# Two-layer attention kernel: sums of the last two blocks shared with VectorE, first two blocks without transferred taps, new order places

## The chip, the cores and the metric

The kernel runs on one core of one Trainium2 chip. The metric is device time in microseconds, as the median of several executions. The names used are those of the profile: PE is TensorE (PEld its weight loads), DVE is VectorE, ACT is ScalarE, POOL is GpSimd, and SP is the engine whose queue issues most of the DMAs.

## The reference, cut to what matters

The input x is a batch of 4 images of 192 channels and 128 x 128 pixels, in float32. Two layers follow each other.

The first layer makes four groups of 192 channels with a 1x1 convolution and a depthwise 3x3 convolution. It forms attention between channels (8 heads of 24 channels, sums over all pixels), applies it to the values, adds x and a gate that comes from the pooled fourth group, and projects with a 1x1 convolution.

The second layer is the one that the change touches:

```
x = x + depthwise3x3(x) + bias
q, k, v = 1x1 convolution of x          (3 dilations: 1, 2, 3; 2 heads of 32 channels each)
scores  = q . k at the 3x3 neighbours   (reflected at the edges, dilated)
weights = softmax over the 9 neighbours
out     = sum over the 9 neighbours of weight * v
out     = 1x1 projection of the three dilations together
```

## The kernel before, in words

The program has two passes. The first one projects x and stores q, k and v of the first layer, then computes the channel attention head by head on PE. The end of that part is the matrix `mix1`, `mix2` (attention and projection multiplied together). It ends in the profile at about 1638 us. The change leaves all of this as it is.

The second pass (`second_pass`) does the rest. Its work is cut into 64 blocks: a block n is 4 rows of 128 pixels of two images, which lie side by side in the 128 partitions where the channels need it. There are 32 blocks for each pair of images. For each block:

- `loads`: SP loads x and v of the first layer (buffers `xv`). `h_product` multiplies them on PE, `h_evict` moves the result from PSUM into ring buffers of 12 rows (`hboth`, `hring2`) on ACT.
- `plan_conv`: the depthwise 3x3 convolution. Channels 0 to 127 of both images lie in `hboth`. `centre` (ACT) makes the middle tap into a PSUM tile `pa`; six taps (`SUMMED` = 0, 1, 2, 6, 7, 5) are added one after the other on DVE (`tap`, line 924), and the last of them writes the tile `y`. The other two taps (`MOVED` = 3, 8) are made by ACT (`moved`, line 937) and added by two accumulating DMAs that POOL issues (`moved_sum`, line 949): the first adds one tap onto the other, the second adds both onto `y`. The remaining 64 channels of both images (`side`) are made by ACT as nine tiles, summed by two accumulating DMAs (`side_rows`, line 968) and two adds on POOL (`side_sum`, lines 976 and 979) into `y2`.
- `plan_kv` and `plan_scores`: k, v and q on PE. Every one of these takes a product with `y` first and then one with `y2`. ACT evicts k and v into rings (`kring`, `vring`). `prod` (line 1094) multiplies q and k on DVE, `pick_sums` (line 1105) sums over channels on PE.
- `plan_softmax`: a chain through ACT, PE, DVE and POOL that ends in a transposing DMA (`weights`, on SP) into `e_sb`.
- `plan_mixed`: for each of three dilations g and nine neighbours t, PE spreads the weights over the channels (`expand`, line 1227, into two PSUM buffers `ex`), DVE multiplies by v (`term`, line 1233: the first one of a group writes `acc`, the others one of four `term` buffers), and POOL adds the eight terms onto `acc` (`term_sum`, line 1236). Then PE projects (`out_product`, lines 1245 and 1249), ACT evicts and SP stores.

The order of all of this is planned before it is issued. Each step is handed to a `Schedule` with an engine, a rank, an estimated cost, and the steps that it must follow. `order()` plays the work through in time: whenever an engine is free, it takes the step of lowest rank among those that are ready, and the order in which steps are taken is the order in which instructions go into the queues. A rank is the block's number plus a place from the table `PLACES` (a first value, and a step for repeated operations), in blocks. A change of PE's tile shape costs 0.12 us in this plan, and such a step's rank is raised by a penalty (1.6704 blocks), so that equal shapes are taken together. The engines then run their queues in order, and every dependence is a semaphore wait.

Buffers limit how far a step can run ahead: `hold` makes the first use of a buffer wait for the last use of its earlier holder. In this pass there are four `term`, four `acc`, two `ex`, two `pc` (PSUM, used for h, k and v, and the output), and one `moved` and one `side` buffer.

Of the kernel before, what the change touches and what calls it, by code (L numbers as in the profile page):

```python
# [36 lines left out]
class Schedule:  # L37
# [16 lines left out]
    def hold(self, pool, bufs, first, last):  # L54

        self.pools.setdefault((pool, bufs), []).append((first, last))
# [130 lines left out]
def rows3(t):  # L187
# [13 lines left out]

PLACES = {
    "loads": (0.5697, 0),
    "h_product0": (-0.8250, 0),
    "h_evict0": (0.7179, 0),
    "h_product1": (-0.2901, 0),
    "h_evict1": (4.5043, 0),
    "h_product2": (-0.7755, 0),  # L210
    "h_evict2": (-0.2139, 0),
    "centre": (5.7183, 0),
    "tap": (2.8884, 0.19030),
    "moved": (-0.0827, 0),
    "moved_sum0": (3.1492, 0),
    "moved_sum1": (4.7398, 0),
    "side1": (1.2593, 0.00003),
    "side0": (0.7171, 0.00011),
    "side_rows0": (2.1868, 0),
    "side2": (1.6271, 0.00019),  # L220
    "side_rows2": (1.4785, 0),
    "side_sum1": (10.8296, 0),
    "side_sum2": (5.4172, 0),
    "kv0": (1.7866, 0.00185),
    "kvev0": (-0.0330, 0.01478),
    "kv1": (3.2540, 0.00019),
    "kvev1": (-2.0029, 0),
    "kv2": (2.4499, 0),
    "kvev2": (1.1258, 0),
    "query0": (2.8659, 0),  # L230
    "prod0": (2.9696, 0),
    "query1": (3.3887, 0),
    "prod1": (3.0988, 0),
    "query2": (3.4244, 0),
    "prod2": (3.5942, 0),
    "pick0": (3.5728, 0.17857),
    "pick1": (3.9636, 0),
    "evicted_scores": (1.8388, 0),
    "by_pixel": (3.8163, 0),
    "top": (6.6680, 0),  # L240
    "below": (5.0643, 0),
    "exponential": (10.6231, 0),
    "total": (-2.1855, 0),
    "divide": (3.8560, 0),
    "part0": (-5.1709, 0),
    "rest": (-2.3314, 0),
    "part1": (-0.0711, 0),
    "part2": (1.6351, 0),
    "weights": (12.2563, 0),
    "expand": (4.2596, 0),  # L250
    "term": (4.7246, 0),
    "term_sum": (8.9696, 0),
    "out0": (6.1072, 0.00004),
    "outev0": (6.1953, 0),
    "store0": (18.8924, 0),
    "out1": (6.1208, 0),
    "outev1": (7.1247, 0),
    "store1": (9.7231, 0),
}

@with_exitstack
# [549 lines left out]
def second_pass(tc, x, w2, xv_p, mix1, mix2, biases, v_dram, v2_dram, out):  # L811
# [4 lines left out]
    with ExitStack() as ctx:  # L816
# [7 lines left out]
            ),  # L824
            dict(pc=2, ex=2, q=1, pa=1, sc=1),
            dict(xv=xv_p),
            (0.12, 1.6704),
        )
        add, hold, tile_of, tiles = stage.schedule.add, stage.hold, stage.tile, stage.tiles
        fill, read, repeat, written = stage.fill, stage.read, stage.repeat, stage.written  # L830
# [12 lines left out]
            nc.gpsimd.memset(r[:, :, 0 : W + 2 : W + 1], 0.0)  # L843

        def at(name, n, k=0):
            first, step = PLACES[name]
            return n + first + step * k

        mm = nc.tensor.matmul

# [135 lines left out]
        def plan_conv(n):  # L986
            prev = first = add("ACT", at("centre", n), 1.25, (centre, n), latency=0.3)
            for m in range(2):
                read("h", m, n, 0, first)
            for j, t in enumerate(SUMMED):  # L990
                prev = add("DVE", at("tap", n, j), 1.19, (tap, n, t, j == 5), [prev])
                for m in range(2):
                    read("h", m, n, t // 3 - 1, prev)
            hold("pa", first, prev)
            two, mvs = prev, []
            for k, t in enumerate(MOVED):
                mvs.append(add("ACT", at("moved", n, k), 1.15, (moved, n, k, t), mvs[-1:]))
                for m in range(2):
                    read("h", m, n, t // 3 - 1, mvs[k])
            both = summed_by_transfer(at("moved_sum0", n), 4.0, (moved_sum, n, 0), mvs)  # L1000
            both = summed_by_transfer(at("moved_sum1", n), 4.0, (moved_sum, n, 1), [both, two])
            hold("moved", mvs[0], both)
            firsts, sums = {}, []
            for j, ty in enumerate((1, 0, 2)):
                for tx in range(3):
                    sd = add("ACT", at(f"side{ty}", n, tx), 0.72, (side, n, ty, tx), firsts.get(ty, [])[-1:])
                    read("h", 2, n, ty - 1, sd)
                    firsts.setdefault(ty, []).append(sd)
                if j:
                    after = [firsts[1][-1], firsts[ty][-1], *sums[-1:]]  # L1010
                    sums.append(summed_by_transfer(at(f"side_rows{ty}", n), 5.8, (side_rows, n, ty), after))
                    hold("side", firsts[ty][0], sums[-1])
            for tx in (1, 2):
                sums.append(add("POOL", at(f"side_sum{tx}", n), 1.26, (side_sum, n, tx), sums[-1:]))
            hold("middle", firsts[1][0], sums[-1])
            return [sums[-2], two, both, [both, sums[-1]]]
# [212 lines left out]
        def term(n, g, t):  # L1229
            ex = tiles.pop(("ex", n, g, t))  # L1230
            to = tile_of("term", ("term", n, g, t)) if t else tile_of("acc", ("acc", n, g))
            for win, px in windows(vring, RING_V, n, g, t):
                nc.vector.tensor_mul(rows3(to[:, px]), rows3(ex[:, px]), win)  # L1233

        def term_sum(n, g, t):
            nc.gpsimd.tensor_add(tiles["acc", n, g], tiles["acc", n, g], tiles.pop(("term", n, g, t)))  # L1236

        def out_product(n, m, g):

# [24 lines left out]
        def plan_mixed(n, w):  # L1264
            sums, spreads = [], []
            for g in range(NG):
                exs, prev = [], None
                for t in range(NT):
# [5 lines left out]
                    if t == 0:  # L1274
                        first = prev = tm
                        continue
                    prev = add("POOL", at("term_sum", n, k), 1.277, (term_sum, n, g, t), [tm, prev])
                    hold("term", tm, prev)
                spreads += exs
                sums.append((first, prev))  # L1280
# [167 lines left out]
```

## Time and profile before

| what | us |
|---|---|
| median of 3 runs | 4407.45 (4406.96 to 4409.0) |
| the profiled execution | 4406.01 |
| its span, first to last instruction | 4404.2 |
| PE busy in the span | 4289.9 (97%) |
| DVE busy | 3806.3 (86%) |
| POOL busy | 3319.0 (75%) |
| ACT busy | 2593.1 (59%) |

The busy time of an engine is the time in which it ran some instruction; issuing DMAs and waiting do not count. A wait in the profile is put down to what released it last. The chain of work that ended last follows the program back from its last instruction, at each step to what released it. In lists by time, a bracket at the end of a line tells how long the engine was idle before it, and what ended that.

### The profile page before, as it was taken

To read this page: it belongs to the slowest core of one execution; us is meant where nothing else is said; L and a number is where in the kernel's file an instruction comes from. 1 tells how busy PE (TensorE), PEld (TensorE's weight loads), DVE (VectorE), ACT (ScalarE), POOL (GpSimd) and SP (SyncE) were. 2 spreads that over 40 slices of the span, in tenths; PEclk is the share of its full clock that TensorE was granted. 3 is DMA by queue.
4 is the path that set the end of the run, shared out by engine and by line. 5 is a ranking of instruction groups with operands and counts; after the bars stand their busy time and mean duration, and the time that the engine had idled before them with its cause. 6 is when DMAs were issued, how large, how long until landed. Compare 5 with 4: busy or idle time off the path is not lost.

```text
span 4404.2 us, 64532 instructions
## 1 busy us (share of the span) xinstructions
PE 4289.9 (97%) x20608; PEld 1649.0 (37%) x20608; DVE 3806.3 (86%) x5492; ACT 2593.1 (59%) x4858; POOL 3319.0 (75%) x3407
## 2 busy tenths in 40 slices
PE   9999999899999998999999999999999999999996
PEld 3333333354445642333333333333333333333321
DVE  7998889855555546999999999999999999999996
ACT  7888888833333337656656556556566566566531
POOL 6777778811111112999999999999999999999998
PEclk9999999999999999999999999999999999999997
DMA  8777787668887648666566666656565665665521
GB/s 268 245 243 237 230 258 251 198 154 175 178 174 172 143 109 177 131 133 135 126 130 132 126 130 129 136 123 128 127 136 124 131 134 125 133 131 125 116 53 32
DMA packets 502386, 675.81 MB, mean 153 GB/s; under 512 B 138576, under 2 KB 320412, under 8 KB 502048
## 3 DMA queue, kind: packets, MB, share of 16 engines
q1 hardware_dynamic: 464160, 504.94, 43.2%
q0 software_dynamic: 37888, 166.74, 20.9%
q8 instruction: 166, 2.72, 0.3%
q14 instruction: 172, 1.41, 0.1%
HBM read 277.72 MB, written 201.33 MB: 109 GB/s over the span
## 4 chain that ended last, share of the span: by engine, by line
PE 80%; DVE 13%; issue 3%; POOL 2%; DMA 1%; ACT 1%; SPq 0%; DVEq 0%; POOLq 0%; ACTq 0%
PE pc L640 12%; PE sc L1105 9%; PE ex L1227 8%; PE pu L357 8%; PE ph L872 7%; PE pkv L1026 5%; DVE term L1233 4%; PE pu L362 4%; PE gram L712 4%; PE pkv L1029 4%; PE q L1086 4%; PE q L1083 4%; DVE prod L1094 3%; PE pu L490 2%; PE po L1249 2%
## 5 line engine op out<-in xcount | busy, mean ns | idle before, releaser
L1236 POOL TENSOR_TENSOR acc<-acc,term 128x512 f32<-128x512 f32 x1536 | 2034.6, 1330 | 133.0 <-DVE term L1233 45.5
L1233 DVE TENSOR_TENSOR term<-ex,vring 128x512 f32<-128x512 f32 (+2 forms) x1596 | 1000.1, 663 | 55.3 <-PE ex L1227 43.1
L1094 DVE TENSOR_TENSOR prod<-q,kring 128x1536 f32<-128x1536 f32 (+1 forms) x600 | 1007.3, 1688 | 16.8 <-PE q L1083 7.3
L427 POOL TENSOR_TENSOR v_True<-v_True,side 128x512 f32<-128x512 f32 (+1 forms) x512 | 647.9, 1267 | 169.7 <-ACT side L416 141.9
L404 DVE SCALAR_TENSOR_TENSOR pa<-vboth,dwv,pa 128x1024 f32<-128x1024 f32 (+1 forms) x448 | 574.3, 1282 | 76.9 <-ACT pa L397 54.4
L1227 PE MATMUL ex<-e_sb,spread 108*128 108x512 bf16 x1728 | 567.2, 387 | 37.5 <-DVE term L1233 31.2
L627 POOL COPY band<-band 64x384 f32<-64x384 f32 x192 | 95.8, 499 | 563.9 <-DMA band<-in_bands 506.5
L640 PE MATMUL pc<-u,band 64*64 64x508 f32 (+1 forms) x4608 | 518.3, 593 | 1.4 <-ACT ring L386 1.4
L1039 ACT COPY kring<-pkv 64x512 f32<-64x512 f32 x384 | 223.3, 581 | 419.5 <-PE pkv L1029 413.9
L924 DVE SCALAR_TENSOR_TENSOR pa<-hboth,posw,pa 128x1024 f32<-128x1024 f32 (+1 forms) x320 | 408.3, 1276 | 38.8 <-ACT pa L912 19.7
L1105 PE MATMUL sc<-prod,pick 128*32 128x512 f32 x3456 | 428.9, 598 | 1.8 <-DVE prod L1094 1.8
L653 DVE BATCH_NORM_STATS2 stats<-pc 128x6 f32<-128x128 f32 x1440 | 303.0, 283 | 141.1 <-ACT conv L649 141.0
L649 ACT COPY conv<-pc 128x512 f32<-128x512 f32 x384 | 210.6, 587 | 296.9 <-PE pc L640 288.7
L1026 PE MATMUL pkv<-y,wkv 128*128 128x512 f32 x768 | 365.5, 598 | 11.8 <-DMA y<-moved 8.7
L1227 PEld LDWEIGHTS <-spread 108*128 108x128 bf16 x1728 | 133.4, 98 | 647.0 <-issue 626.7
L872 PE MATMUL ph<-xv,mix 128*64 128x512 f32 (+1 forms) x1024 | 374.3, 596 | 0.5 <-DMA mix<-mixed 0.5
L357 PE MATMUL pu<-xt,wx 128*128 128x512 f32 x768 | 366.0, 613 | 8.3 <-DMA xt<-in_x 8.3
L1252 ACT COPY o<-po 128x512 f32<-128x512 f32 x192 | 106.2, 588 | 433.5 <-PE po L1249 227.9
L416 ACT ACTIVATE side<-ring,dwv 128x512 f32<-128x512 f32 (+1 forms) x512 | 350.8, 736 | 13.9 <-POOL v_True L427 13.1
L956 ACT ACTIVATE side<-hring,posw 128x512 f32<-128x512 f32 (+1 forms) x512 | 340.9, 710 | 9.6 <-DMA side<-side 7.7
L640 PEld LDWEIGHTS pc<-u,band 64*64 64x64 f32 x4608 | 189.5, 134 | 301.2 <-issue 284.7
L1039 ACT COPY vring<-pkv 64x512 f32<-64x512 f32 x384 | 223.9, 583 | 45.9 <-PE pkv L1029 32.6
(165 smaller groups left out, 6073.8 us busy)
## 6 DMA issues: line engine op xcount, KB each, us to landing
qk_dram<-us SPq DMA_DIRECT2D x192, 512.0 KB
u<-qk_dram SPq DMA_DIRECT2D x384, 256.0 KB
side<-side POOLq DMA_DIRECT2D x124, 768.0 KB, 7.1
xt<-in_x SPq DMA_DIRECT2D x64, 512.0 KB
v_dram<-v_False SPq DMA_DIRECT2D x64, 512.0 KB
xv<-in_x SPq DMA_DIRECT2D x128, 256.0 KB
xv<-v_dram SPq DMA_DIRECT2D x128, 256.0 KB
y<-moved POOLq DMA_DIRECT2D x64, 512.0 KB, 5.2
```

Source lines behind the costliest of these rows:

```text
L357: mm(pu, wx[:, mt * 128 : (mt + 1) * 128], tiles["xt", n][:, im, :], start=True, stop=False)
L404: nc.vector.scalar_tensor_tensor(by_row(to[:, o : o + length]), by_row(vboth[:, at : at + length, :, t % 3 : t % 3 + W]), dwv[:, 0, t : t ...
L427: nc.gpsimd.tensor_add(v[:, rows, :], v[:, rows, :], z[:, rows, :])
L640: nc.tensor.matmul(pcs[e][r * G : (r + 1) * G, :, to], band[at, e, c, dx, :], u[at, e, c, :].rearrange("p (b w) -> p b w", w=W)[:, :, of], ...
L872: mm(to, w[:, cols], tiles["xv", n, j, im], start=j == 0, stop=j == 2)
L1026: mm(rows3(tile_of("pc", key)), w, tiles["y", n, im], start=True, stop=False)
L1039: nc.scalar.copy(rows[HALVES[im], :, pad : pad + W], rows3(tiles["pkv", n, pair, im])[HALVES[e]])
L1094: nc.vector.tensor_mul(to[:, :, px].rearrange("p t (r w) -> p t r w", w=W), q.unsqueeze(1).to_broadcast([128, 3, *q.shape[1:]]), three,)
L1105: mm(sc[quad * 32 : (quad + 1) * 32, :], pick[:, QR - 4 * row : QR - 4 * row + 32], tiles["prod", n, k // NT, k % NT // 3][:, k % 3, :], s ...
L1227: mm(rows3(tile_of("ex", ("ex", n, g, t))), spread[:, t, :], e_sb, start=True, stop=True)
L1233: nc.vector.tensor_mul(rows3(to[:, px]), rows3(ex[:, px]), win)
L1236: nc.gpsimd.tensor_add(tiles["acc", n, g], tiles["acc", n, g], tiles.pop(("term", n, g, t)))
```

## The change

There are three parts, all in the second pass.

1. In blocks 0 and 1, the taps 3 and 8 are no longer made on ACT and added by transfers. DVE adds them between its fifth and its last tap, so it does eight taps there instead of six.
2. In blocks 62 and 63, the sums of the neighbours t = 6, 7 and 8 of each dilation are made on DVE instead of POOL (`helped`): 3 x 3 x 2 = 18 sums. The plan prices one at 0.60 us instead of 1.277.
3. All places in the table are replaced. Each gets two more values: for blocks 0 to 3 the first is added (4 - n) times, and for blocks 60 to 63 the second is added (n - 59) times. The penalty for a change of shape becomes 2.2447.

```diff
-    "loads": (0.5697, 0),
-    "h_product0": (-0.8250, 0),
-    "h_evict0": (0.7179, 0),
-    "h_product1": (-0.2901, 0),
-    "h_evict1": (4.5043, 0),
...
-    "tap": (2.8884, 0.19030),
-    "moved": (-0.0827, 0),
...
-    "side_sum1": (10.8296, 0),
-    "kv0": (1.7866, 0.00185),
-    "prod0": (2.9696, 0),
-    "evicted_scores": (1.8388, 0),
-    "below": (5.0643, 0),
-    "part0": (-5.1709, 0),
-    "rest": (-2.3314, 0),
-    "term": (4.7246, 0),
-    "term_sum": (8.9696, 0),
-    "store0": (18.8924, 0),
...
+    "loads": (3.2117, 0, -0.1081, -0.1768),
+    "h_product0": (-1.0791, 0, -0.2172, 0.0738),
+    "h_evict0": (-1.5681, 0, 0.4291, 0.7768),
+    "h_product1": (-0.4538, 0, -0.1272, -0.2531),
+    "h_evict1": (2.9139, 0, -1.1902, 0.4891),
...
+    "tap": (3.0287, 0.15354, -0.1279, -0.1148),
+    "side_sum1": (12.5101, 0, 0.4347, 0.0454),
+    "kv0": (1.6801, 0, 0.0023, -0.1926),
+    "prod0": (3.1190, 0, -0.0092, -0.0614),
+    "evicted_scores": (3.4729, 0, 0.2114, -0.4090),
+    "below": (3.6315, 0, 0.3421, -0.3529),
+    "part0": (-7.1206, 0, 0.7557, 0.1340),
+    "rest": (-4.3348, 0, -0.2530, -0.1376),
+    "term": (3.3951, 0, 0.2670, -0.1634),
+    "term_sum": (13.4212, 0, -0.3796, -0.0967),
+    "store0": (15.2417, 0, -0.7670, 0.0550),
+    "moved": (-0.1229, 0, 0.8936, -0.5433),
...
-            (0.12, 1.6704),
+            (0.12, 2.2447),
...
         def at(name, n, k=0):
-            first, step = PLACES[name]
-            return n + first + step * k
+            first, step, early, late = PLACES[name]
+            u = n + first + step * k
+            if n < 4:
+                u += early * (4 - n)
+            if 2 * NB - 1 - n < 4:
+                u += late * (4 - (2 * NB - 1 - n))
+            return u
...
-            for j, t in enumerate(SUMMED):
-                prev = add("DVE", at("tap", n, j), 1.19, (tap, n, t, j == 5), [prev])
+            early = n < 2
+            on_vector = SUMMED[:5] + MOVED + SUMMED[5:] if early else SUMMED
+            for j, t in enumerate(on_vector):
+                prev = add("DVE", at("tap", n, j), 1.19, (tap, n, t, t == SUMMED[5]), [prev])
...
-            two, mvs = prev, []
-            for k, t in enumerate(MOVED):
-                mvs.append(add("ACT", at("moved", n, k), 1.15, (moved, n, k, t), mvs[-1:]))
...
+            two, both, mvs = prev, prev, []
+            if not early:
+                for k, t in enumerate(MOVED):
+                    mvs.append(add("ACT", at("moved", n, k), 1.15, (moved, n, k, t), mvs[-1:]))
...
+        def helped(n, g, t):
+
+            return n >= 2 * NB - 2 and t >= 6
+
         def term_sum(n, g, t):
-            nc.gpsimd.tensor_add(tiles["acc", n, g], tiles["acc", n, g], tiles.pop(("term", n, g, t)))
+            engine = nc.vector if helped(n, g, t) else nc.gpsimd
+            engine.tensor_add(tiles["acc", n, g], tiles["acc", n, g], tiles.pop(("term", n, g, t)))
...
-                    prev = add("POOL", at("term_sum", n, k), 1.277, (term_sum, n, g, t), [tm, prev])
+                    engine, us = ("DVE", 0.60) if helped(n, g, t) else ("POOL", 1.277)
+                    prev = add(engine, at("term_sum", n, k), us, (term_sum, n, g, t), [tm, prev])
```

## The prediction

> **What bounds the kernel now.** I read the busy times by stretch first, then the chain that ended last, then both ends in order of time, then groups and waits. The stretches of the second pass (columns: length, then busy us and instructions of PE, PEld, DVE, ACT, POOL, then the granted PE clock, DMA share, GB/s):
>
> ```profile
> 1626.00:1800.00 174.00, 151.46 (x558) 50.44 (x558) 114.08 (x141) 120.59 (x225) 69.10 (x68) 0.94 0.71 155
> 1800.00:4200.00 2400.00, 2378.62 (x9970) 846.45 (x9968) 2361.97 (x2704) 1436.45 (x2806) 2260.06 (x1905) 1.00 0.61 129
> 4200.00:4280.00 80.00, 74.05 (x307) 23.65 (x309) 75.88 (x91) 27.90 (x67) 73.76 (x62) 0.96 0.21 46
> 4280.00:4391.00 111.00, 80.92 (x273) 22.78 (x265) 81.03 (x129) 12.32 (x27) 105.31 (x85) 0.79 0.11 29
> ```
>
> From 1800 to 4200 PE is busy 99.1% and DVE 98.4%. A block takes about 41.65 us there (three blocks lie between the ph products at 2063.88 and 2188.81 in the chain), so 2,400 us are 57.6 blocks with 0.37 us of PE idle each. The change takes no PE work away. All that a new order can win in the middle is 21.4 us, in practice much less, but it can lose any amount. At the ends PE idles 22.5 us in the first stretch, and the last two stretches hold 36 us. There the two structural edits act.
>
> The start, from the chain and from POOL's own list:
>
> ```profile
> 1660.29 1.29 DVE y L924
> 1661.60 1.22 ACT pa L912
> ...
> 1665.72 9.14 DMA y<-moved
> 1675.00 3.63 PE pkv L1026 x4
> 1678.63 1.06 PE pkv L1029 x4
> ```
>
> ```profile
> 1659.09 0.89 POOL L949 DMA_DIRECT2D moved<-moved  x1 [7.56 <-ACT moved L937]
> 1660.91 0.85 POOL L968 DMA_DIRECT2D side<-side  x1 [0.93 <-ACT side L956]
> 1665.72 0.85 POOL L949 DMA_DIRECT2D y<-moved  x1 [3.96 <-DVE pa L924]
> 1671.34 1.26 POOL L976 TENSOR_TENSOR y<-side 128x512 f32<-128x512 f32 x1 [4.76 <-DMA side<-side]
> 1672.68 1.26 POOL L979 TENSOR_TENSOR y<-y,side 128x512 f32<-128x512 f32 x1
> ```
>
> Block 0's y leaves DVE at 1661.6 but is complete only when the transfer lands at 1674.9; PE stands 8.68 us. Right behind it is a second path: the side channels (y2), summed by two transfers and two POOL adds, end at 1673.94.
>
> The tail, from POOL's list and the waits after 4280 (total us, times, longest):
>
> ```profile
> 4280.00 20.08 POOL L1236 TENSOR_TENSOR acc<-acc,term 128x512 f32<-128x512 f32 x15
> ...
> 4308.67 22.64 POOL L1236 TENSOR_TENSOR acc<-acc,term 128x512 f32<-128x512 f32 x17
> ...
> 4336.55 54.40 POOL L1236 TENSOR_TENSOR acc<-acc,term 128x512 f32<-128x512 f32 x41
> ```
>
> ```profile
> DVE term L1233 <- POOL acc L1236: 11.1, 18, 1.5
> ```
>
> POOL runs 79 sums and six softmax steps almost without a gap until 4390.95. DVE has slack (81.0 us busy) and waits for POOL to free term buffers. PE's last out products follow at 4391.0, and the rest to 4404.2 is a fixed 13 us.
>
> **What the Trainium skill says.** "SBUF — State Buffer", section "Who interferes with whom": a VectorE instruction with two SBUF inputs contends with a GpSimd instruction that reads SBUF, and the later one is held until the other ends. The second pass of the kernel before has no row where this meets: term and prod read one operand from PSUM (ex, q), tap reads pa there. So no run here shows it yet, and I bound it below. "GPSIMD Engine Reference", section "3. Performance versus the Vector engine", gives a two-input add as 1.96 times slower on GpSimd; here it is 1267 ns on POOL against 722 ns for the nearest VectorE row with SBUF operands, 1.75 times:
>
> ```profile
> L701 DVE TENSOR_TENSOR square<-cutT 128x512 f32<-128x512 f32 x8 | 5.8, 722 | 16.5 <-ACT cutT L699 16.5
> ```
>
> "TensorE: Matmul & The Clock Gate", section "What's actually happening": PE falls to half clock after an idle window. The trace agrees: after the 8.68 us wait four pkv matmuls take 3.63 us, in the middle 1.72.
>
> **The change, part by part.** The sum is made against the profiled execution, 4406.01 us (span 4404.2 and 1.8 around it); the median of the three runs is 1.44 above it.
>
> *First two blocks without transferred taps.* Removed: 4 ACT taps of 1.14 us (4.6), 4 accumulating transfers of 512 KB, 4 issues of about 0.87 us on POOL's queue (3.5). Added: 4 DVE taps of 1.28 us (5.1), bare DVE time in a stretch where DVE idles 60 us; without that cover they cost 5.1. y of block 0 is then ready near 1661.6 + 2 x 1.3 = 1664.2 instead of 1674.9, 10.7 earlier. That is not the gain, for y2 is late next: the second product of each pair (L1029) needs it, and behind that instruction PE's queue holds the other pairs and the queries. y2 is ready at 1673.94; the first ACT tap in front of the sides is gone (1.15), POOL's issue in front of side_rows is gone, and two transfers fewer share the DMA engines, which are over-full (share 1.07 from 1665 to 1675). I bound y2 between 1673.9 and 1669. The first pair's L1029 starts at 1678.56 before, so block 0 gains 4.6 to 9.5. Block 1 has its y<-moved issue at 1687.16 behind side_rows, and PE then waits 2.97 us at 1698.10 and runs slow again (3.00 instead of 1.72): up to 4 us more, at the least nothing. After that the ramp is paced by PE itself and by the first e_sb transpose at 1744.91, so a part is lost again. Bounds 3 and 13; I take **-7**.
>
> *Last two blocks' sums.* t = 6, 7, 8 of three groups and two blocks are 18 sums. POOL loses 18 x 1.34 (its pitch, 54.40/41 = 1.33, and the step) = 24.1 us. DVE gains 18 x 0.72 = 13.0. Upper end: without contention DVE holds 81.0 + 13.0 = 94.0 us from 4280, POOL 111.0 - 24.1 = 86.9, so DVE becomes the bound, the last sum ends no earlier than 4374, and 17 us are won at most. Lower end: with contention each DVE sum first lets POOL's running sum end (half of 1.27, 0.63), so DVE holds 81.0 + 18 x 1.35 = 105.3 and wins 5.7; POOL is held 13.0 and ends 11 earlier. Queued behind a waiting DVE sum are terms, which PE's expands (two ex buffers) wait for. The sums' place is 13.4 blocks behind their own, later than all other DVE work, so in the plan they fill DVE's holes and do not push terms. I take **-10**. If DVE had no holes, the 13.0 would stand on its path in full.
>
> *Order anew.* All places move and two get terms for four blocks at either end; the penalty for a change of PE's tile shape goes from 1.6704 to 2.2447. No instruction is added. In the middle most places stay near the old (kv, query, prod within 0.4 block), while h_evict1, below, evicted_scores, part0, rest, side_sum and term_sum move by 1 to 4.5. These are small ACT, POOL and DVE steps; on SP only loads and stores move (loads 2.6 blocks later, store0 3.7 earlier), and SP's queue is far from full. The trace cannot say what order comes out, so the bounds are -8 (PE's idle falls by a third) and +26 (0.45 us a block, worked out below). I take **0**.
>
> Sum: 4406.0 - 7 - 10 = 4389.0, as a median **4390.4, so 4390 us**.
>
> **The rivals.**
>
> *The middle loses its cover (slower).* PE's idle is 0.37 us a block because expand and term hand two ex buffers back and forth with hardly a stall: from 1800 to 4200 terms wait 29.0 us for expands and expands 13.5 for terms. If the new places put one more prod (1.66 us) ahead of a due term, the next expand and what stands behind it on PE wait. At 17/57.6 = 0.30 us a block the gain of both ends is gone; at 0.45 the time is 4406 - 17 + 26 = 4415, a median of 4416. For it: three engines over 94% busy. Against it: the heavy places hardly moved.
>
> *Moved sums give nothing.* DVE sums stand for POOL and POOL for them, terms come late, and the tail's gain is 0 to 4. Then only the start is left: 4406 - 7 - 2, a median of 4398. For it: both operands lie in SBUF. Against it: DVE waits for POOL there anyway, so some of its standing is free.
>
> *Both ends at their full worth.* -12 at the start, -17 at the tail, -6 in the middle: 4371, a median of 4372. For it: separate end places. Against it: DVE would need to be full from 4280 on.
>
> *The ends' edits do not act.* Were y not on PE's path, the start would give nothing, but the chain shows the transfer there; this is within the cases above.
>
> **How the numbers follow.** Forecast 0.54 (own range 4380 to 4398), moved sums worthless 0.18, full worth 0.11, middle slower 0.17. Within 0.2% is 8.8 us, 4398.6 to 4416.3: what a measurement of this kernel can hardly tell from none. The forecast gives 0.49 faster and 0.05 same; worthless sums 0.09 and 0.08 and 0.01 slower; full worth 0.11 faster; the slow middle 0.02 same and 0.15 slower. Together 0.69, 0.15, 0.16. The range 4368 to 4413 takes in the full worth and most of the small losses.
>
> **What would show it.** Start: no y<-moved before block 2, PE's wait before the first pkv under 3 us or moved to L1029, first expand near 1747 instead of 1753.7. Tail: 18 POOL sums fewer and 18 acc<-acc,term rows on DVE; their mean tells the contention (0.72 is none, 1.35 the lower end); last sum 6 to 17 us nearer to the steady stretch's end. Middle: PE idle of 0.9% as before. The prediction is wrong if PE's idle in the middle passes 1.6% (0.30 us a block more), or if DVE sums last over 2 us.

## The result, and the profile after

The changed kernel takes 4411.48 us (median of 13 runs, 4408.91 to 4415.85) against 4407.45 us for the kernel before on the same chip (13 runs): a ratio of 1.001, with a 95% interval of 1.0001 to 1.0019. By the bound of 0.2% that is no change; the interval lies above 1, so what difference there is, about 4 us, is a loss. The forecast was 4390, with a range up to 4413. The expected gain of 17 us did not arrive.

The profiled execution of the changed kernel took 4415.85 us (span 4414.1), 9.9 more in span than before. Of these, 3.3 lie in the first pass, which the change leaves alone: the last row of the channel attention's sums over pixels (`gram`) starts at 1609.09 instead of 1605.82. Over all profiled executions of this study this start spreads by 5.3 us, though no kernel changes anything before it. So below all starts are "net", that is, less the difference to the kernel before.

The busy times by stretch of the changed kernel (columns as in the prediction: length, then busy us and instructions of PE, PEld, DVE, ACT, POOL, then clock, DMA share, GB/s):

```profile
1626.00:1800.00 174.00, 157.32 (x590) 53.42 (x589) 121.30 (x146) 114.05 (x214) 63.82 (x62) 0.94 0.63 141
1800.00:4200.00 2400.00, 2378.16 (x9919) 842.32 (x9917) 2347.14 (x2689) 1419.45 (x2791) 2248.86 (x1895) 1.00 0.60 128
4200.00:4280.00 80.00, 75.34 (x314) 25.05 (x313) 77.32 (x92) 33.67 (x82) 76.84 (x64) 1.00 0.30 62
4280.00:4401.00 121.00, 90.68 (x320) 25.20 (x320) 104.04 (x160) 16.54 (x36) 98.43 (x77) 0.81 0.12 30
```

The first row shows the gain at the start: PE is busy 157.3 instead of 151.5 us. The last one, which like the one before it ends with the last sum, shows the tail's edit: DVE works 104.0 instead of 81.0 us, POOL 98.4 instead of 105.3 (some of it work that was done before 4280 in the kernel before). In the second row PE's share is the same 99.1% as before, but fewer PE and DVE instructions fit into the same 2400 us (9919 and 2689, instead of 9970 and 2704). So the middle is slower, and PE's idle time doesn't show it.

To see it, one must hold the work constant, not the time. A good mark is DVE's first softmax step of a block (`mx<-st`). Between those of blocks 11 and 54 lie 43 blocks, in the kernel before and in the one after:

```profile
2186.58:3977.79 1791.21, 1774.28 (x7440) 632.11 (x7439) 1761.05 (x2028) 1072.09 (x2094) 1685.63 (x1420) 1.00 0.62 130
```

```profile
2187.27:3986.67 1799.40, 1783.72 (x7441) 632.23 (x7441) 1759.61 (x2028) 1064.46 (x2094) 1685.20 (x1420) 1.00 0.60 129
```

The same number of instructions of DVE, ACT and POOL takes 8.2 us longer, 0.19 a block in the mean. DVE and POOL work no longer on them, but PE is "busy" 9.4 us longer with the same number of matmuls (one record in 7440 apart).

From mark to mark the profiled execution of after stands to before like this (us):

| stretch | before | after | difference |
|---|---|---|---|
| last `gram` row to block 9 | 497.03 | 494.48 | -2.55 |
| block 9 to block 57 | 1999.25 | 2009.23 | +9.98 |
| block 57 to block 63 | 223.55 | 226.80 | +3.25 |
| block 63 to the end of the span | 78.55 | 74.50 | -4.05 |

Both ends gain, though less than half of what was forecast, and the stretch between takes all of it back.

At the start, PE's own list for the changed kernel (the lines left out don't wait):

```profile
1667.28 1.08 PE L1095 MATMUL q<-y,wq 128*64 128x512 f32 x4 [1.02 <-DVE y L930]
...
1673.29 1.12 PE L1092 MATMUL q<-y,wq 128*128 128x512 f32 x2 [0.26 <-POOL y L985]
1674.35 1.13 PE L1038 MATMUL pkv<-y,wkv 64*128 64x512 f32 x4
1677.92 1.17 PE L878 MATMUL ph<-xv,wp 128*128 128x512 f32 x2 [2.44 <-ACT kring L1048]
```

The wait of 8.68 us for the transfer onto `y` is gone. What is left are 1.02 us for DVE's `y`, 0.26 for POOL's `y2`, and 2.44 for ACT, which evicts k and v. The first pair's second product (now L1038) starts at 1674.35, net 1671.1, instead of 1678.56: 7.5 us earlier.

In the tail, POOL's list and DVE's list for one dilation of block 63:

```profile
4351.55 3.95 POOL L1250 TENSOR_TENSOR acc<-acc,term 128x512 f32<-128x512 f32 x3
4358.12 7.30 POOL L1250 TENSOR_TENSOR acc<-acc,term 128x512 f32<-128x512 f32 x5 [2.62 <-DVE term L1242]
4368.02 1.64 POOL L1250 TENSOR_TENSOR acc<-acc,term 128x512 f32<-128x512 f32 x1 [2.60 <-DVE term L1242]
...
4381.48 6.97 POOL L1250 TENSOR_TENSOR acc<-acc,term 128x512 f32<-128x512 f32 x5 [5.02 <-DVE acc L1242]
```

```profile
4356.76 0.68 DVE L1250 TENSOR_TENSOR acc<-acc,term 128x512 f32<-128x512 f32 x1
4357.35 1.28 DVE L1242 TENSOR_TENSOR term<-ex,vring 128x512 f32<-128x512 f32 x2
4358.55 1.38 DVE L1250 TENSOR_TENSOR acc<-acc,term 128x512 f32<-128x512 f32 x1
4359.85 0.68 DVE L1242 TENSOR_TENSOR term<-ex,vring 128x512 f32<-128x512 f32 x1
4360.45 1.15 DVE L1250 TENSOR_TENSOR acc<-acc,term 128x512 f32<-128x512 f32 x1
4361.52 1.27 DVE L1242 TENSOR_TENSOR term<-ex,vring 128x512 f32<-128x512 f32 x2
4364.38 2.13 DVE L1242 TENSOR_TENSOR term<-ex,vring 128x512 f32<-128x512 f32 x3 [1.58 <-PE ex L1236]
```

POOL, almost without a gap before, now stands up to 5.0 us at a time and waits for DVE. DVE stands only 1.58 us per dilation. A dilation (first term to first term of the next) hardly gets shorter: the last one of block 62 took 10.6 us and takes 10.9, the one before it 11.05 and 11.0. From the first term of block 62 to the last sum, the six dilations take 65.1 us instead of 68.6. A DVE sum takes 0.68 to 0.69 us alone, and 0.88 to 1.38 in 7 of the 8 cases in which it starts while a POOL instruction runs. A POOL sum that starts while a DVE sum runs takes 1.58 to 1.71 instead of 1.27.

### The profile page after: what moved, and what is told of

It is laid out like the page before. It is cut to its first block, busy times and chain, and to the rows that moved or that the text cites. A ratio compares the mean times of both kernels' runs of the same rounds, so it can differ in the third digit from the quotient of the medians.

```text
span 4414.1 us, 64329 instructions
## 1 busy us (share of the span) xinstructions
PE 4305.7 (98%) x20608; PEld 1647.6 (37%) x20608; DVE 3822.8 (87%) x5514; ACT 2581.1 (58%) x4854; POOL 3299.7 (75%) x3385
## 4 chain that ended last, share of the span: by engine, by line
PE 81%; DVE 10%; POOL 4%; issue 4%; ACT 1%; DMA 1%; SPq 0%; DVEq 0%; POOLq 0%; ACTq 0%
PE pc L641 12%; PE ph L878 8%; PE ex L1236 8%; PE pu L358 8%; PE sc L1114 8%; PE pkv L1035 5%; PE pu L363 4%; PE gram L713 4%; PE po L1263 4%; DVE term L1242 4%; PE q L1095 3%; PE pkv L1038 3%; PE q L1092 3%; PE po L1259 3%; POOL acc L1250 3%
## 5 line engine op out<-in xcount | busy, mean ns | idle before, releaser
L1250 POOL TENSOR_TENSOR acc<-acc,term 128x512 f32<-128x512 f32 x1518 | 2020.1, 1338 | 145.2 <-DVE term L1242 62.2
L962 ACT ACTIVATE side<-hring,posw 128x512 f32<-128x512 f32 (+1 forms) x512 | 337.4, 709 | 11.7 <-DMA side<-side 10.1
```

The source lines that it names most:

```text
L1250: engine.tensor_add(tiles["acc", n, g], tiles["acc", n, g], tiles.pop(("term", n, g, t)))
```

## Experiments

### Which of the three parts gains, and which loses

Theory A is that of the forecast for the ends, with the new order taking their gain back in the middle. Four kernels take the change apart. "Old places" means that `PLACES` of before is used with end terms of zero and the penalty of 1.6704.

```
e1_old_taps    old places;  early = n < 2 (kept);   helped: n >= 2 * NB (never)
e2_old_sums    old places;  early = n < 0 (never);  helped: n >= 2 * NB - 2 and t >= 6 (kept)
e3_old_both    old places;  both kept
e4_order_only  new places;  both off
```

> The kernel before with the old places and penalty; only blocks 0 and 1 get eight taps on DVE and no transferred ones. Theory A (both edits gain, the new order in the middle takes it back): 2 to 6 us faster than before, and PE's wait before the first pkv under 5 us instead of 8.7. Theory B (the edits gain nothing, since side channels or the ramp are late next): within 1.5 us of before. Theory C (an edit loses): slower by over 2 us.

> The kernel before with the old places and penalty; only the 18 sums of blocks 62 and 63 go to DVE. Theory A: 4 to 10 us faster than before. Theory B: within 2 us. Theory C (DVE sums stand behind POOL's and hold up the terms): slower by over 2 us; DVE sums then last 1.1 us or more in the mean instead of 0.68.

> Both edits with the old places and penalty: what is left of the change without its new order. Theory A: 6 to 16 us faster than before, so 10 to 20 under the changed kernel. Theory B: as before within 2 us. Theory C: as the changed kernel, 3 to 6 us slower than before.

> The new places and penalty alone; transferred taps in all blocks and all sums on POOL as before. Theory A: 10 to 20 us slower than before, with the blocks between 5 and 57 taking 0.15 to 0.3 us each longer. Theory B: 3 to 6 us slower than before, as the changed kernel. Theory C: as before or faster.

| kernel | median us (before: 4406.54) | ratio, 95% interval | net start to block 9, less before | blocks 11 to 54 (before: 1791.2) | block 63 to end (before: 78.55) |
|---|---|---|---|---|---|
| taps alone | 4403.84 | 0.9992, 0.9983 to 1.0000 | -1.5 | 1790.8 | 78.7 |
| sums alone | 4403.91 | 0.9993, 0.9984 to 1.0001 | +1.3 | 1791.6 | 74.2 |
| both, old places | 4401.33 | 0.9987, 0.9980 to 0.9993 | -1.4 | 1790.8 | 74.9 |
| order alone | 4425.95 | 1.0045, 1.0032 to 1.0058 | +15.9 | 1796.4 | 76.0 |

With the old places the two edits gain 5.2 us together. Each alone gains about 2.7, with an interval that reaches 1. The new order alone loses 19.4 us. So A has the sign right for both edits together and for the order. It expected more of the sums (4 to 10) and of both (6 to 16). The start's marks are not sharp: the kernel with the sums alone leaves the start as it was, and still stands at +1.3 there.

The order's loss has two parts. Some 5 us are in the middle, and 16 at the start, where PE stands twice for `y` (the first bracket names ACT, but the transfer onto `y` that POOL issues at 1664.03 lands at 1672.28):

```profile
1672.42 3.75 PE L1035 MATMUL pkv<-y,wkv 128*128 128x512 f32 x4 [8.04 <-ACT side L962]
...
1696.64 3.75 PE L1035 MATMUL pkv<-y,wkv 128*128 128x512 f32 x4 [4.87 <-DMA y<-moved]
```

These two waits are not the 16 us, though. The kernel before stands at the same two products, for 8.68 and 2.97 us, and in the net stretch from 1626 to 1703 PE is busy for 57.5 us in both. The loss comes behind it: from there to block 9, PE idles 13.2 us instead of 5.1, most of it for terms, and is busy 7.7 us longer. In the changed kernel the taps' edit is worth 18 us at block 9 (+15.9 to -2.55), of which 16 only make good what the new order had lost. Why the new order needs this edit was not tested.

Why are the taps worth 1.5 us alone and not 7? The chain of work that ended last, for the kernel with the taps alone:

```profile
1661.44 8.43 DMA side<-side
1669.87 0.07 issue
1669.94 1.28 POOL y L982
1671.22 0.07 issue
1671.29 1.27 POOL y L985
1672.56 0.04 issue
1672.61 2.08 PE q L1092 x2
```

As the prediction said, `y2` is late next, by the transfer of 8.43 us. PE waits 2.78 us there, and the first expand starts at net 1747.3 instead of 1753.7; the prediction had put it near 1747. But at block 5 only a part is left: in the 130 us after the first pass PE is busy 5.4 us longer than before (113.5 against 108.1), in the 70 us behind them 2.6 us less (66.3 against 69.0). The ramp gives back what the first block had won. Which of the later steps sets its pace was not tested.

### Is y2 really next

In the kernel with both edits and old places, the side channels of blocks 0 and 1 too go to DVE: one ACT tile, then eight DVE taps, no transfers and no POOL adds.

```
+ if n < 2:
+     side0 = prev = add("ACT", at("side1", n), 0.72, (side_first, n))
      ...
+     for j, t in enumerate((3, 5, 0, 1, 2, 6, 7, 8)):
+         prev = add("DVE", at("tap", n, j) + 0.005, 0.60, (side_tap, n, t), [prev])
          ...
+     return [side0, two, both, [both, prev]]
```

> As e3, and in blocks 0 and 1 also the side channels are summed on DVE (eight taps of one ACT tile) without transfers and POOL adds. Theory that y2 was the next late input at the start: PE's wait before the first pkv and q products (2.78 us in e1 plus cold clock) is gone, the first expand comes 3 to 6 us nearer to the end of the first pass, and the total is 2 to 5 us under e3 (4396 to 4399). Rival (whatever the start wins is given back in blocks 2 to 5, where PE and DVE are full): first expand earlier, total as e3 within 1.5 us.

It took 4398.47 us (before: 4407.32; ratio 0.9982, 0.9974 to 0.9991). PE's list:

```profile
1663.85 1.97 PE L1121 MATMUL q<-y,wq 128*64 128x512 f32 x4 [4.36 <-DVE y L930]
1665.75 2.08 PE L1118 MATMUL q<-y,wq 128*128 128x512 f32 x2
...
1672.80 1.13 PE L1064 MATMUL pkv<-y,wkv 64*128 64x512 f32 x4
```

The wait for `y2` is gone; the first one left is for DVE's `y`. The first pair's second product (L1064) is hardly sooner for it (net 4.1 us ahead of before's L1029, against 3.9 with the taps' edit alone), since other products now stand in front of it, but block 9 is net 3.5 us earlier than before, against 1.4. The first expand was expected 3 to 6 us nearer than with both edits alone, and came 1.2 nearer (net 1746.2 against 1747.4). So `y2` was next, and worth some 2 us by the marks, which are no sharper than 1.3; by the medians' ratios, 0.9982 and 0.9987, the two kernels can't be told apart.

### Is the tail's gain lost to contention

DVE's sums read two operands from SBUF. In one kernel, both edits with the old places, the helped terms stay in PSUM (`to = ex`, released only after the sum), so each DVE sum reads one operand from SBUF:

```
+ if helped(n, g, t):
+     to = tiles["term", n, g, t] = ex
  ...
- hold("ex", exs[-1], tm)
+ if not helped(n, g, t):
+     hold("ex", exs[-1], tm)
  ...
- hold("term", tm, prev)
+ if helped(n, g, t):
+     hold("ex", exs[-1], prev)
+ else:
+     hold("term", tm, prev)
```

> Both edits with old places and penalty (as e3), but the helped terms stay in their PSUM buffer ex, so that a DVE sum reads one operand from PSUM and one from SBUF. Contention theory (a DVE sum with two SBUF operands and a POOL sum hold each other up): DVE sums last 0.75 us at most and POOL sums 1.30 at most, where e2 has up to 1.40 and 1.71; the tail is 3 to 6 us shorter than e3's, so 4396 to 4399. Rival (a long DVE sum only waits for the result of POOL's sum before it): lasts as long as before, time as e3 (4401) or later, since ex buffers are held longer.

Durations of the sums at one source line, in the kernel with the sums alone, and with the helped terms in PSUM (ns, minimum/median/maximum):

```profile
L1250 POOL TENSOR_TENSOR acc<-acc,term x88: 1259/1272/1714, 4240.6 to 4384.6; 128x512 f32<-128x512 f32 x88
...
L1250 DVE TENSOR_TENSOR acc<-acc,term x18: 678/691/1403, 4334.4 to 4388.7; 128x512 f32<-128x512 f32 x18
```

```profile
L1253 POOL TENSOR_TENSOR acc<-acc,term x86: 1262/1272/1295, 4239.5 to 4386.5; 128x512 f32<-128x512 f32 x86
...
L1253 DVE TENSOR_TENSOR acc<-acc,ex x18: 675/686/690, 4330.6 to 4390.6; 128x512 f32<-128x512 f32 x18
```

The long sums are gone: none of the 18 lasts over 0.69 us and no POOL sum over 1.30. By itself this doesn't show that the second SBUF operand made them long, for in this kernel no DVE sum runs beside a POOL sum any more. One runs beside a POOL softmax step, for 0.68 us, where its like with the sums alone took 1.40.

The other traces show more. In the changed kernel all 7 DVE sums over 0.75 us started while a POOL instruction ran. All 10 POOL sums over 1.40 us in the tail started while a DVE sum ran, and none of the 15 shorter ones beside them did. And DVE's terms, which read one operand from PSUM, don't stretch: of those of full size in the kernel before, 1342 run for half of their time or more beside a POOL sum and take 0.685 us in the median, and 203 run beside none and take 0.682. So that the two SBUF operands are what makes the sums long rests on these overlaps.

The time did not fall: 4404.26 us (before: 4407.32; 0.9994, 0.9985 to 1.0002), where both edits alone had 0.9987 and 4396 to 4399 us were expected. The two `ex` buffers are now held until the sums end, and PE's expands wait 14.5 us for these sums, where with the sums alone only out products wait for them. So contention is there, but taking it away in this manner brings a new wait, and what it costs in time stays open. In the changed kernel it makes DVE's 18 sums 3.4 us longer in all.

### How much should DVE take, and what it waits for

Four kernels on top of the one with the side channels on DVE: only two sums of eight instead of three; the same for three blocks; and for both divisions, the out products of one dilation put behind the next dilation's expands, since DVE's 1.58 us are waits for expands that stand behind an out product on PE.

```
e9    return n >= 2 * NB - 2 and t >= 7     (12 sums)
e12   return n >= 2 * NB - 3 and t >= 7     (18 sums)
e13   t >= 6, and in plan_mixed:
      + if n >= 2 * NB - 2 and g + 1 < NG:
      +     after.append(spreads[NT * (g + 1) + NT - 1])
e14   t >= 7, with the same two lines
```

> As e6, but only t = 7 and 8 of each dilation go to DVE in the last two blocks (12 sums instead of 18). Theory that three sums of eight only moved the bound of a group from POOL (8 x 1.34 = 10.7 us) to DVE (10.9 us in e2): with two, POOL has 6 x 1.34 = 8.0 and DVE about 9, a group takes 9 to 9.6 us, and the total is 4 to 9 us under e6 (4390 to 4394). Rival (the end is set by what comes before it, the weights of block 63): within 1.5 us of e6 (4397 to 4400).

> As e9, with the last three blocks helped (18 sums). If POOL's backlog from block 61 sets the end: 2 to 5 us under e9. If DVE, full until about 4280, sets it: as e9 or up to 4 us over it.

> As e6, but in the last two blocks the out products of a dilation come after the nine expands of the next dilation. If the product ahead of the expands holds up DVE: the waits of 1.58 us before a term go to under 0.7, a group in the last two blocks takes 9.5 us instead of 10.9, and the total is 3 to 7 us under e6 (4391 to 4396). If the long DVE sums are the limit: within 1.5 us of e6.

> As e9 (12 sums on DVE) with the out products behind the next dilation's expands. If the product ahead of the expands holds up DVE: 3 to 7 us under e9 (4391 to 4395). If not: within 1.5 us of e9.

| kernel | median us (before on the same chip) | ratio, 95% interval | last dilation of block 62, us | first term of block 62 to last sum (before: 68.6; 18 sums: 64.0) |
|---|---|---|---|---|
| 12 sums | 4397.61 (4408.13) | 0.9976, 0.9966 to 0.9985 | 10.5 | 62.2 |
| 18 sums of three blocks | 4404.18 (4408.13) | 0.9994, 0.9986 to 1.0002 | | 64.9 |
| 18 sums, out products later | 4400.80 (4406.10) | 0.9986, 0.9979 to 0.9992 | 11.3 | 65.6 |
| 12 sums, out products later | 4397.02 (4406.10) | 0.9981, 0.9973 to 0.9989 | 10.1 | 63.9 |

The kernel with 12 sums has the lowest ratio of this study, below those of before and after, though its gain over 18 sums is smaller than the 4 to 9 us that were expected (0.9976 against 0.9982, on different chips, with intervals that overlap). With 12 sums POOL has little of the holes that 18 leave it; the largest is left at the last dilation:

```profile
4339.44 8.65 POOL L1276 TENSOR_TENSOR acc<-acc,term 128x512 f32<-128x512 f32 x6 [0.55 <-DVE term L1268]
4349.35 8.64 POOL L1276 TENSOR_TENSOR acc<-acc,term 128x512 f32<-128x512 f32 x6 [1.26 <-DVE term L1268]
4361.47 16.90 POOL L1276 TENSOR_TENSOR acc<-acc,term 128x512 f32<-128x512 f32 x12 [3.48 <-DVE acc L1268]
```

Helping a third block costs 6.6 us, more than was expected. DVE has no room for block 61's sums (from 4200 to 4280 it is busy 76.9 of 80 us with them and without), and block 62's first term starts 5.7 us later. Moving the out products gained nothing in the total. With 18 sums the wait only moved, to 1.79 us before the first term of a dilation. That the place of the out product alone sets the tail is refuted. What remains, and is argued from the lists but not shown by a run, is DVE's own chain: nine terms and three sums in order, beside POOL's sums, with four `term` and two `ex` buffers.

### What makes the middle longer

First the parts of the new order: the penalty, the end terms, and the two halves of the table.

```
e7    the changed kernel with (0.12, 1.6704)
e8    both edits, old places, with (0.12, 2.2447)
e15   the changed kernel with all end terms 0
e10   both edits, old places, but new ones for loads, h, centre, tap, moved, side, kv
e11   both edits, old places, but new ones for everything else, query to store
```

> The changed kernel with the old penalty of 1.6704. If the higher penalty makes the middle slower: blocks 9 to 57 at the pace of before, total 6 to 10 us under the changed kernel (4402 to 4406). If the places do it: as the changed kernel, 4408 to 4415, with blocks 9 to 57 still 7 to 10 us longer in sum than before.

> As e3 (both edits, old places) with the new penalty of 2.2447. If the penalty makes the middle slower: 6 to 10 us over e3 (4407 to 4411). If the places do it: within 3 us of e3.

> The changed kernel with the two end values of every place set to 0. If the end values help the ends: 5 to 20 us slower than the changed kernel, with blocks 9 to 57 at the changed kernel's pace (8 us more in sum than before). If they are a part of the loss: faster than the changed kernel.

> As e3 (both edits, old penalty, no extra values at the ends), with the new places for loads, h, convolution, side and k and v only; the rest keeps the old places. If these places are the slow ones: blocks 11 to 57 take 7 to 10 us more in sum than with the old places. If the others are: 0 to 2 us more.

> As e3, with the new places for query, prod, pick, softmax, terms, sums and output only. If these places are the slow ones: blocks 11 to 57 take 7 to 10 us more in sum than with the old places. If the others are: 0 to 2 us more. If both halves are near 0, only the two together are slow.

| kernel | median us (before on the same chip) | ratio, 95% interval | blocks 11 to 54 |
|---|---|---|---|
| new places, old penalty | 4412.30 (4407.32) | 1.0012, 1.0004 to 1.0020 | 1798.6 |
| old places, new penalty | 4401.95 (4407.32) | 0.9989, 0.9982 to 0.9995 | 1791.0 |
| new places, no end terms | 4416.09 (4406.10) | 1.0022, 1.0014 to 1.0031 | 1798.8 |
| front half new | 4623.61 (4408.13) | 1.0506, 1.0483 to 1.0528 | 1971.9 |
| back half new | 4503.26 (4408.13) | 1.0218, 1.0204 to 1.0232 | 1873.8 |

All kernels with the old places lie between 1790.8 and 1792.2 us for blocks 11 to 54, those with the whole new table between 1796.4 and 1799.4, whatever the penalty, the end terms and the edits. So the places are the cause; this is shown. The end terms help the ends (without them the ratio is 1.0022 instead of 1.0010, some 5 us; block 63 to the end takes 79.7 us instead of 74.5) and have no part in the loss. Halves of the table could not tell which places: each half alone is far worse than both. With the front half alone ACT waits 143.6 us for the scores between 2400 and 3600, and POOL 89.2 us for side channels.

Then a place that stands out in TensorE's own lists. In the changed kernel and in those with the order alone, the old penalty, no end terms or a shift of 0.1 (below), the 128*128 out products (L1259) mostly come directly behind score products of shape 128*32 between blocks 11 and 57 (32 to 40 times in 46 blocks). In the one before and the one with both edits and old places they never do: an expand comes behind these score products, and the out products come behind the transpose of the scores (`st`). First from the changed kernel, then from the kernel before:

```profile
3019.79 1.06 PE L1114 MATMUL sc<-prod,pick 128*32 128x512 f32 x6
3020.78 1.13 PE L1259 MATMUL po<-acc,wo 128*128 128x512 f32 x2
```

```profile
3010.69 1.06 PE L1105 MATMUL sc<-prod,pick 128*32 128x512 f32 x6
3011.68 0.61 PE L1227 MATMUL ex<-e_sb,spread 108*128 108x512 bf16 x2
```

The step looked like the loss: 37 times in blocks 11 to 54, at an estimated 0.3 us beyond what the score products themselves take, it would be worth 11 us. The waits of PEld in that stretch seemed to say why (total us, times, longest), in the changed kernel and in the one before:

```profile
PEld po L1259 <- ACT o L1266: 24.3, 29, 0.8
...
PEld po L1263 <- POOL acc L1250: 21.9, 38, 1.4
```

```profile
PEld po L1249 <- POOL acc L1236: 6.6, 28, 0.2
```

PEld waits with the weights of L1259 until ACT has evicted the product before it. But the two lists above have the same 0.99 us from the first line's start to the second's. Whatever follows the last score product of a group starts 0.52 to 0.53 us after it, all 129 times in the kernel before and all 130 times in the changed one. So the step from the score products costs no more than the one in its place before. The wait shows a little later, between L1259's own products: their distances are 3.2 us longer in all than before, not 11. Three kernels test what the step is worth. Two take it away, one leaves it as a control:

```
e16   "out0": 5.7377 -> 5.9377, "out1": 5.7872 -> 5.9872
e17   "out0": 5.7377 -> 5.8377, "out1": 5.7872 -> 5.8872
e18   "out1": 5.7872 -> 5.9372
```

> The changed kernel with the places of the out products alone put 0.2 of a block later (5.7377 to 5.9377 and 5.7872 to 5.9872); nothing else differs. In TensorE's order of the second pass the first 128*128 out product (L1259) then follows the transpose of the scores, as in the kernel before, instead of score products of shape 128*32. Theory A (the loss in the middle lies in that place: 38 times in 46 blocks the step from the score products to L1259 costs about 0.3 us, with L1259's weight load waiting for ScalarE to evict the out product before it): the waits of L1259's loads for ScalarE vanish, blocks 11 to 57 take 1915 to 1919 us instead of 1925.5, and the time is 6 to 10 us below the changed kernel's, 4402 to 4406. Theory B (the loss is spread over all moved places, the step only makes visible time that would be lost elsewhere): the middle stays within 3 us of 1925 and the time within 3 us of 4411.

> The same two places, but 0.1 of a block later only: TensorE's order changes a little, and the score products stay directly ahead of L1259 as in the changed kernel. It is the control for the run with 0.2: Theory A expects no gain, blocks 11 to 57 within 3 us of 1925.5 and the time within 3 us of the changed kernel's 4411. Were any small shift to help, it would gain as the 0.2 does.

> The changed kernel with only the place of the 128*128 out products (L1259) 0.15 later (5.7872 to 5.9372): the score products no longer stand ahead of them, an expand or a ph product does. Theory A: as with both moved by 0.2, the waits for ScalarE's eviction vanish and most of the 10 us in the middle comes back, 4402 to 4407. Theory B: within 3 us of 4411.

| kernel | median us (before: 4406.66) | ratio, 95% interval | scores directly before L1259 | blocks 11 to 54 |
|---|---|---|---|---|
| both 0.2 later | 4450.44 | 1.0097, 1.0084 to 1.0111 | 0 times | 1807.0 |
| both 0.1 later | 4413.18 | 1.0016, 1.0009 to 1.0022 | 37 times | 1799.2 |
| second 0.15 later | 4449.92 | 1.0093, 1.0079 to 1.0107 | 0 times | 1825.9 |

The step is gone in two of them, and with it L1259's waits for ACT, as Theory A said (with the second place alone moved, the weights of ph products wait 23.5 us for the same evictions). The distances between L1259's products are short again, by 3.2 and 4.0 us in all. But the middle got longer, so Theory A falls with the size that it gave the step. The control leaves PE's order from block 11 to 54 exactly as in the changed kernel, and stays at its time; so it says nothing about small shifts that do change the order. The expectations name blocks 11 to 57. There the three take 1926.7, 1918.9 and 1951.5 us, the changed kernel 1925.5; but with both places moved, the first softmax step of block 57 itself has shifted against its neighbours by 5 us or more, so the shorter stretch is shown. The rest of the slow-down is at the end, where the kernel with 0.2 needs 95.8 us from block 63's softmax on, not 74.5.

What PE does with the time shows when all its matmuls from block 11 to 54 are sorted by which follows which, start to start. Apart from waits, the distance hardly depends on anything else. Call 128*128 and 108*128 large shapes, and 64*128, 128*64 and 128*32 small ones. The next matmul starts 0.43 us after a 128*128 product on 512 columns if it is large, and 0.52 if it is small; after an expand these are 0.22 and 0.31; and after the last of a group of small ones 0.52. PE goes from large to small 350 times in the kernel before, 377 times in the changed one, and 387 and 386 times in the first and the last of the three. With every pair at its usual distance, the changed kernel's sequence takes an estimated 3.5 to 4 us longer than the one before, about half of the loss, and that with both places 0.2 later about 6 us longer, of 16 in all. The rest are distances longer than usual. In the changed kernel they grow most between out products (5.7 us, L1259's 3.2 among them) and shrink most from k and v products to expands (6.4 us). The profile counts them as busy.

**What stays open** is which of the 54 places makes the middle longer. What is known: it is not PE's idle time, and not DVE's or POOL's work. PE's matmuls are the same, but change more often to a small shape, which is about half of the loss by the distances above; no run tests that half alone. A further table with single places moved wasn't tried, and neither was a fresh search for places that fit both edits.

## Why the prediction was wrong

**"Order anew: I take 0" failed.** Its bounds were -8 and +26. The measured value is +10 between blocks 9 and 57, and +19 for the order without the edits. The reason given was that the heavy places hardly move, and that small ACT, POOL and DVE steps do not matter. The first half misreads the table: `term`, 27 products of DVE in each block, moves 1.33 blocks earlier, and `term_sum`, counted there among the small steps, is POOL's main work (24 sums of 1.27 us in a block of 41.65) and moves 4.45 later. And the sum has no term for PE's own sequence, since no instruction was added. But the new order has PE go from large to small shapes 377 times instead of 350 in blocks 11 to 54, and with the usual distances that makes about half of the 8.2 us there; the other half are longer distances between the same matmuls. Which places did it is not known.

**The rival "the middle loses its cover" had the right sign and the wrong mechanism.** It put the deciding point at 0.30 us a block, and 0.19 to 0.21 came. That was enough because the ends gained less. So that the measured 4411.48 lies near the 4416 of this rival, and inside the stated range, is in part luck. (That 4416 lies inside the band up to 4416.3 that the prediction calls the same, so its 0.15 for slower didn't fit its own figure.) It expected PE to wait for terms, but those waits fell, from 11.0 to 6.4 us in blocks 11 to 54. The sign named for it, PE's idle above 1.6%, never came: PE idles 0.9% in the middle, as before. What lasts longer is counted as busy. The test itself was blind to the loss.

**The start, -7, was over-sized.** The mechanism is right in each step: the wait of 8.68 us for the transfer gone, `y2` late next, the first expand at net 1747.3 where 1747 was predicted (under the old places; under the new ones it is net 1753.2). The term that failed is "a part is lost again": of the 6.4 us at the first expand, 1.5 are left at block 9 with the old places, and 2.55 came in the changed kernel, by marks that are sharp to 1.3.

**The tail, -10, was over-sized.** 18 sums moved as said and POOL lost its 24 us. The bounds of a DVE sum, 0.72 and 1.35 us, nearly hold: 0.68 to 0.69 alone, up to 1.38 beside a POOL sum, 0.88 in the mean. The missed term is the pace: the sum asked when each engine would have done its total, 94 to 105 us, but DVE's chain is in order and waits 1.58 us per dilation for expands and up to 1.15 for POOL. So the six dilations of the last two blocks take 65.1 us where they took 68.6. The last stretch is 4.05 us shorter, 6 less than said. The rival "moved sums give nothing" (0 to 4) was nearly right here. By DVE's list its waits for expands weigh more (10.0 us from 4335 on) than the stretching of its sums (3.4 us); no run parts the two.

The Trainium skill, "SBUF — State Buffer", section "Who interferes with whom", says that a VectorE instruction with two SBUF inputs contends with a GpSimd instruction that reads SBUF. The prediction had no row for it and bounded it. The traces agree: in the changed kernel DVE sums take up to 1.38 us against 0.68 to 0.69 alone, and POOL sums up to 1.71 against 1.27, while terms with one operand in PSUM take 0.685 us beside a POOL sum and 0.682 alone. As the prediction had it from that page, each time the later of the two is held.

The sum that came: -2.6 at the start, +10.0 and +3.3 between blocks 9 and 63, -4.1 at the end. That is +6.6 in the profiled execution, beside +4.0 between the medians.

## What to carry to other kernels

When an order is replaced, compare equal work from mark to mark, not PE's idle share: a list-scheduled kernel can lose time in which PE counts as busy. Count how often each order changes between large and small matmul shapes. Places in such a list work as a set; here half of the new table cost 2% and 5%, and one place moved by 0.15 of a block cost 0.8%. An edit that frees a bound engine should be tried with the old order first: here that was 0.13% faster, and with the side channels and fewer moved sums 0.24%, while with the new order nothing of it was left.

## What the runs showed of the hardware

Not expected was how evenly the contention is paid. In alternation each engine becomes the later one: a VectorE sum that starts beside a GpSimd instruction goes from 0.69 us to 0.88 to 1.40, and a GpSimd sum that starts beside a VectorE sum from 1.27 to 1.58 to 1.71, so moving one sum can cost POOL 0.4 us as well. And the same matmuls can take 9.4 us more of TensorE's busy time over 1791 us, at full granted clock in both. A step from a large to a small shape stood 0.09 us above one that stays large (0.52 against 0.43 us, 0.31 against 0.22), and the order decided how many there were (377 instead of 350).
